# A GRU over 128 steps: the input products of the last four steps made plainly, with the input weights loaded a second time

## The chip, the cores and the metric

The kernel runs on one core of a Trainium2 chip. The core has TensorE (PE: matrix products, with PEld for loading the stationary operand), VectorE (DVE), ScalarE (ACT), GpSimd (POOL) and SyncE (SP, which here only issues DMAs). The metric is the device time of one execution in microseconds (us).

## The reference

`x` has 64 rows, 128 steps and 512 values; `h` starts as `cond_1024` (64 x 512). Everything is float32.

```python
def step(h, inp):
    x_t, prop = inp
    comb = jnp.concatenate([x_t, h], axis=-1)
    z = jax.nn.sigmoid(comb @ Wz + bz)
    r = jax.nn.sigmoid(comb @ Wr + br)
    comb2 = jnp.concatenate([x_t, r * h], axis=-1)
    h_cand = jnp.tanh(comb2 @ Wh + bh)
    h_new = (1.0 - z) * h + z * h_cand
    h_next = jnp.where(prop, jnp.tanh(h_new @ Wp + bp), h_new)
    return (h_next, h_new)
```

`prop` holds in every fourth step but the last one (steps 3, 7, ..., 123). The output is `x` plus the `h_new` of every step. Each of Wz, Wr, Wh has 1024 rows: the upper 512 multiply `x_t`, the lower 512 multiply `h` or `r * h`.

## The kernel before

**Layout.** The 64 rows and two halves of the 512 columns make 128 partitions: a state tile is 128 x 256. A product with a 512 x 512 weight is four k blocks of 128 (`K`), and each block is two matmuls, one for each half of the columns (`products`, L174, L177). I call one such pair of matmuls a unit. In the trace a float32 matmul leaves two records, so a unit leaves four. `ORDER` is 0, 2, 1, 3: the blocks of the first column half of the turned state come first.

**One step** (the loop at L557). The sums of R, Z and H live in PSUM slots, in two tiles: `rc` holds R and H, `zp` holds Z and the prop product. Each slot is seeded with the step's input part and bias by an ACT copy out of `G[t]` (`seed`, L382), and the h products add to it. The order on TensorE is: R (eight matmuls), Z (eight), the turns (transposes, L202, four records for each column half) of `rh`, x units from a queue (`fill`), H (eight, from `rhT`), x units, the turn of the new h's first half, x units, the second turn, x units. In a prop step the product with Wp, a second tanh and two more turns follow, again with x units between. Between these products stand: sigmoid on ACT (L598) and r*h on DVE (L599); the copies of turned tiles out of PSUM (L193); z, its complement and keep = (1-z)*h (L613 to L615); tanh on ACT (L637), times z (L638) and plus keep (L643) on DVE.

**The x part.** For steps 8 to 127 the products x @ W are made for eight steps at once (two groups of four steps) with two nested levels of a seven-product scheme for 2 x 2 blocks (Winograd's form of Strassen's). A group needs 49 products of 128 x 192 columns in place of 64. `batches` (L473) lists the 14 outer products of two groups and makes seven batches of two; a batch has 14 units. Their sums are read out of PSUM by ACT and DVE (`end_1`, `end_2`), and the outer sums that give `G[t]` are made on POOL (`outer_1` to `outer_c21`). The scheme's operands are sums: `sum_raw12` and its like make them from x on POOL, and those of the weights are made once, in steps 0 to 3, partly **in place** in `wx` (L304 to L314). After that `wx` no longer holds the input weights, except for its k block 3. Steps 1 to 7 use `plain` (L401): twelve units of 256 columns a step, read out by two DVE adds.

**What sets the order.** The program is written in the order in which each engine runs (`manual_schedule`). The number of x units at each place of a step is fixed by `PLACES`, with a period of eight steps: `fill(n)` takes n units from `queue`; a batch's read-out waits in `pending` until the next `read_out()`. The last call, `batches(30)` at step 114, covers groups 30 and 31 (steps 120 to 127); its 98 units are used up in step 122. Steps 123 to 127 have no x units. In step 127 half of Z is placed behind the turns of rh (L603 to L610).

**DMAs.** SP loads x group by group, turns it for TensorE by a DMA transpose (L253), and stores four steps of output at a time (L733).

Of the kernel before, what the change touches and what calls it, by code (L numbers as in the profile page):

```python
# [17 lines left out]
def kernel(  # L18
# [29 lines left out]
    nc = tc.nc  # L48
# [7 lines left out]
    Q4 = 4  # L56
    CHUNK = 4
    FIRST = 2
    R, Z, H_ = range(3)
    assert B * S == P and D == H and T % 8 == 0  # L60

# [93 lines left out]
    def cut(ps):  # L155
        return ps.rearrange("p (c n) -> p c n", c=C)
# [29 lines left out]
    def product(ps, lT, w, k, start=False):  # L186
        s0, c0 = divmod(k, C)
        products(ps, lT[:, c0, ts(s0, B)], lambda s: w[:, k, ts(s, N)], start)
# [37 lines left out]
    def turn_x(t, eng=nc.scalar):  # L226
        g, i = divmod(t, Q4)
        new_xT(g)
        src = xr[g] if g < 2 else early[g]
        for c in range(C):  # L230
            turn(src[:, i, :], xT[g][:, i], c, f"xT_{t}", eng)
# [96 lines left out]
    def sum_raw12(g):  # L328
        v = xT[g]
        sx[g, 12] = one.tile([P, 4, C, B], F32, tag="s12r", name=f"s12r_{g}")  # L330
        four([sx[g, 12][:, n] for n in range(4)], v[:, 0], v[:, 1])
# [6 lines left out]
    def sum_s12(g):  # L338
        v = xT[g]
        o = sx[g, "o12"] = one.tile([P, 2, 2, P], F32, tag="o12", name=f"o12_{g}")  # L340
        nc.gpsimd.tensor_add(o[:, 0], v[:, 2:4, 0, :], v[:, 2:4, 1, :])
        nc.gpsimd.tensor_sub(o[:, 1], o[:, 0], v[:, 0:2, 0, :])
        s = sx[g, 56] = one.tile([P, 4, 2, B], F32, tag="s56", name=f"s56_{g}")
        four([s[:, n] for n in range(4)], o[:, :, 0], o[:, :, 1])

    def sum_s34(g):
        v = xT[g]
        o = sx[g, "o34"] = one.tile([P, 2, 2, P], F32, tag="o34", name=f"o34_{g}")
        nc.gpsimd.tensor_sub(o[:, 0], v[:, 0:2, 0, :], v[:, 2:4, 0, :])
        nc.gpsimd.tensor_sub(o[:, 1], v[:, 0:2, 1, :], sx[g, "o12"][:, 1])  # L350
        s = sx[g, 73] = one.tile([P, 4, 2, B], F32, tag="s73", name=f"s73_{g}")
        four([s[:, n] for n in range(4)], o[:, :, 0], o[:, :, 1])
# [23 lines left out]
    def new_cp(q):  # L376
        if q not in cp:
            cp[q] = one.tile([P, C, 2, 3, P], F32, tag=f"cp{q % 2}", name=f"cp_{q}")
            for b in range(2):
                G[2 * q + b] = cp[q][:, :, b]  # L380

    def seed(i, t):  # L382
        if t < T:
            nc.scalar.copy(cut(slots[i]), G[t][:, :, i, :])  # L384
# [5 lines left out]
    def fill(n):  # L390
        for _ in range(min(n, len(queue))):
            unit, end = queue.pop(0)
            unit()
            if end is not None:
                pending.append(end)
# [5 lines left out]
    def plain(t):  # L401
# [20 lines left out]
        ]  # L422
        return [(u, None) for u in units[:-1]] + [(units[-1], end)]

    MB = {}

    def batch(n, ms):

        def region(ps, m):
            return ps[:, m].rearrange("p g u -> p (g u)")  # L430

        def unit(ps, m, j, start):
            g, i = ms[m]
            products(
                region(ps, m), lhs(g, i, j), lambda s: factor(i, j)[:, s], start and m == 0
            )

        def units(ps, j, start):
            return [lambda m=m: unit(ps, m, j, start) for m in range(2)]

        def blocks():
            return MB[n].rearrange("p m b g (a u) -> p m b a g u", a=2)

        def end_1():
            MB[n] = mbp.tile([P, 2, 2, 3, P], F32, tag="mb", name=f"mb_{ms[0][0]}_{ms[0][1]}")
            for m, (g, i) in enumerate(ms):
                M[g, i] = MB[n][:, m]
            T2[n] = one.tile([P, 2, 3, P // 2], F32, tag="cx", name=f"cx_{ms[0][0]}_{ms[0][1]}")
            q1 = one.tile([P, 2, 3, P // 2], F32, tag="cq", name=f"cq_{ms[0][0]}_{ms[0][1]}")
            nc.scalar.copy(T2[n], x_ps)  # L450
            nc.scalar.copy(q1, q_ps)
            nc.vector.tensor_add(T2[n], r_ps, T2[n])  # L452
            nc.vector.tensor_add(blocks()[:, :, 0, 0], a_ps, q1)

        def end_2():
            q2 = one.tile([P, 2, 3, P // 2], F32, tag="cq", name=f"cq2_{ms[0][0]}_{ms[0][1]}")
            nc.scalar.copy(q2, q_ps)  # L457
            nc.vector.tensor_add(blocks()[:, :, 0, 1], r_ps, q2)  # L458
            nc.vector.tensor_add(blocks()[:, :, 1, 0], x_ps, q2)
            nc.vector.tensor_add(blocks()[:, :, 1, 1], q_ps, T2[n])  # L460

        free = units(a_ps, 2, True)
        one_ = units(q_ps, 1, True) + units(r_ps, 5, True) + units(x_ps, 7, True)
        two_ = units(x_ps, 4, False) + units(q_ps, 6, False) + units(r_ps, 3, False)
        seq = [(u, None) for u in free + one_ + two_]
        seq[7] = (seq[7][0], end_1)
        seq[13] = (seq[13][0], end_2)
        return seq

    M = {}  # L470
# [2 lines left out]
    def batches(g):  # L473

        if g * Q4 >= T:
            return []
        ms = [(g, i) for i in (1, 2, 6, 5, 7, 3, 4)] + [(g + 1, i) for i in (1, 6, 2, 5, 3, 7, 4)]
        return sum((batch((g, n), ms[2 * n : 2 * n + 2]) for n in range(7)), [])


    def flat(v):
# [18 lines left out]
    def outer_1(g):  # L500
        with_bias(g, 1, bias0)
# [27 lines left out]
    )  # L529


    turn_x(0, nc.vector)
    turn_x(1, nc.vector)
    h = h_init
# [22 lines left out]
    for t in range(T):  # L557
# [7 lines left out]
        if t < 3:  # L565
            queue.extend(plain(2 * t + 2) + plain(2 * t + 3))
            places = (12, 12)
        elif t == 3:
            queue.extend(batches(FIRST))
            places = (8, 8, 6)  # L570
        elif u == 7:

            queue.extend(batches(even + 2))


        for k in ORDER:
# [11 lines left out]
            turn_x(2 * t + 6)  # L588
            turn_x(2 * t + 7)
        read_out()  # L590
        if u == 0 and pair >= 1:
            outer_u2(odd - 2)
        if t == 3:
            for i in (1, 2, 3):
# [5 lines left out]
        seed(R, t + 1)  # L600


        for k in ORDER[: 2 if last else K]:  # L603
            product(slots[Z], hT, wh[Z], k)
        rhT = new_T("rhT", f"rhT_{t}")
        for c in range(C):
            turn(rh, rhT, c, f"rhT_{t}", nc.vector)
        if last:
            for k in ORDER[2:]:
                product(slots[Z], hT, wh[Z], k)  # L610
        z = two.tile([P, N], F32, tag="z", name=f"z_{t}")
        keep = two.tile([P, N], F32, tag="keep", name=f"keep_{t}")
        nc.scalar.activation(z, slots[Z], AF.Sigmoid)  # L613
# [4 lines left out]
            nc.scalar.copy(cut(slot_p), bias[:, :, 3, :])  # L618
        if last:
            nc.gpsimd.tensor_add(xr[g][:, j, :], xr[g][:, j, :], keep)  # L620
        fill(places[0])


        for k in ORDER:
# [10 lines left out]
        for c in range(C):  # L635
# [5 lines left out]
                nc.vector.tensor_add(o, pc, o)  # L641
                continue
            nc.vector.tensor_add(h_new[:, ts(c, P)], pc, keep[:, ts(c, P)])  # L643
        seed(H_, t + 1)
        read_out()
        fill(places[1] - 3 if places[1] > 6 else 4)
        h = h_new
        if not last:
            hT = new_T("hT", f"hT_{t}")
            turn(h, hT, 0, f"hT_{t}", nc.vector)  # L650
            fill(1)
            turn(h, hT, 1, f"hT_{t}", nc.scalar)
        fill(2 if places[1] > 6 else 1)
        if t == 2:
            sum_outer_1()
        if t == 3:
# [2 lines left out]
        if prop:  # L659
            for k in ORDER:  # L660
                product(slot_p, hT, wp, k)
            read_out()
            h = two.tile([P, N], F32, tag="hprop", name=f"hprop_{t}")
            for c in range(C):
                nc.scalar.activation(h[:, ts(c, P)], slot_p[:, ts(c, P)], AF.Tanh)
            fill(places[2] - 2)
            hT = new_T("hT", f"hpT_{t}")
            for c in range(C):
                turn(h, hT, c, f"hpT_{t}", (nc.vector, nc.scalar)[c])
            fill(2)  # L670
        if t == 0:
            turn_x(4)
            turn_x(5)
# [3 lines left out]


        if pair >= 0:
            if u == 0 and pair >= 1:  # L680
                outer_c22(odd - 2)
                outer_c21(odd - 2)
            if here:
                if u == 0:
                    sum_s34(even)
                    outer_1(even)
                elif u == 1:
                    outer_c11(even)
                    sum_raw12(odd)
                elif u == 2:  # L690
                    outer_u1(even)
                    outer_5(even)
                    sum_raw4(even)
                elif u == 3:
                    outer_c12(even)
                    outer_u2(even)
                    outer_c22(even)
                    sum_s12(odd)
                elif u == 4:
                    outer_c21(even)  # L700
                    outer_1(odd)
                    sum_s34(odd)
                elif u == 5:
                    outer_u1(odd)
                    outer_c11(odd)
                    sum_raw4(odd)
                elif u == 7:
                    outer_5(odd)
                    outer_c12(odd)
        if u == 7 and pair >= -1 and (even + 2) * Q4 < T:  # L710
# [11 lines left out]
            nc.gpsimd.tensor_add(xr[g][:, j, :], xr[g][:, j, :], h_new)  # L722


        n = 0
        if t >= T - CHUNK:
            n = {T - 2: 3, T - 1: 1}.get(t, 0)
# [60 lines left out]
```

## Time and profile before

| | us |
|---|---|
| median of 3 runs (lowest to highest) | 1371.43 (1371.06 to 1373.5) |
| profiled execution, device time | 1370.75 |
| its span, first to last instruction | 1368.9 |
| TensorE busy | 1342.6 |
| GpSimd busy | 938.7 |

The last steps, each counted from its first R product to the next step's (the last one to the end of the span), with the x units placed in it:

| step | start | length | x units |
|---|---|---|---|
| 117 | 1262.27 | 9.67 | 12 |
| 118 | 1271.94 | 8.56 | 8 |
| 119 (prop) | 1280.50 | 14.09 | 20 |
| 120 | 1294.59 | 8.44 | 8 |
| 121 | 1303.03 | 8.44 | 8 |
| 122 | 1311.47 | 9.88 | 12 |
| 123 (prop) | 1321.35 | 11.53 | 0 |
| 124 | 1332.88 | 8.44 | 0 |
| 125 | 1341.32 | 8.44 | 0 |
| 126 | 1349.76 | 8.44 | 0 |
| 127 | 1358.20 | 10.70 | 0 |

A timeline line reads: start, duration of the merged group, engine, line and operation, output<-input, shape, how many records; in brackets, how long the engine sat idle before it and what released it. The ends of matmuls are modelled, so lengths on TensorE are best read from start to start. In the slices, a digit is the busy share of one fortieth of the span in tenths.

### The profile page before, as it was taken

How to read it: one execution, taken by the hardware profiler on the slowest of the kernel's cores; microseconds unless marked ns; L12 is line 12 of the kernel's file. 1: busy time of each engine (PE TensorE's matmuls, PEld its weight loads, DVE VectorE, ACT ScalarE, POOL GpSimd, SP SyncE). 2: the span in 40 equal slices, each digit the busy share in tenths (PEclk: the TensorE clock that was granted, in tenths of full speed). 3: DMA queues.
4: the chain of work that ended last, by engine and by line, in shares of the span. 5: the costliest groups of instructions: out<-in, count | busy, mean ns of one | idle time of the engine just before them, and what ended most of it. 6: DMA issues, size and time to landing. Idle time of an engine off the chain costs nothing.

```text
span 1368.9 us, 37448 instructions
## 1 busy us (share of the span) xinstructions
PE 1342.6 (98%) x15336; PEld 1028.9 (75%) x15336; DVE 689.2 (50%) x1875; ACT 631.2 (46%) x1857; POOL 938.7 (69%) x1139
## 2 busy tenths in 40 slices
PE   7999999999999999999999999999999999999996
PEld 4777777777777777777777777777777777777764
DVE  4245554555555555554555555555555555555543
ACT  1234445445444445445445444445445445454443
POOL 4327676787767786677686767786677686767740
PEclk9999999999999999999999999999999999999999
DMA  9002212212231222212222131222212222131010
GB/s 286 11 17 48 63 32 63 63 33 63 49 77 32 60 36 63 63 32 63 52 43 63 43 83 34 49 46 63 63 32 63 48 48 63 35 76 33 17 33 16
DMA packets 113572, 73.86 MB, mean 54 GB/s; under 512 B 61556, under 2 KB 109812, under 8 KB 113400
## 3 DMA queue, kind: packets, MB, share of 16 engines
q1 hardware_dynamic: 112336, 69.68, 22.5%
q8 instruction: 121, 1.98, 0.6%
q10 hardware_dynamic: 1064, 1.78, 0.4%
q14 instruction: 51, 0.42, 0.1%
HBM read 39.99 MB, written 16.78 MB: 41 GB/s over the span
## 4 chain that ended last, share of the span: by engine, by line
PE 96%; DMA 2%; DVE 1%; ACT 0%; issue 0%; SPq 0%; DVEq 0%; ACTq 0%
PE rc L177 33%; PE zp L177 20%; PE scratch_q L177 11%; PE scratch_x L177 10%; PE scratch_r L177 10%; PE turn L202 6%; PE scratch_a L177 6%; DMA early<-in_x_dram 1%; DMA wx<-in_L_cond_Wz_dram 1%; DMA wh<-in_L_cond_Wr_dram 1%; DVE h L643 0%; DVE turn L638 0%; ACT xT L193 0%; SPq L93 0%; DVE tw L300 0%
## 5 line engine op out<-in xcount | busy, mean ns | idle before, releaser
L177 PE MATMUL rc<-wh,rhT 128*64 128x256 f32 x2048 | 246.6, 381 | 2.0 <-ACT zp L614 2.0
L485 POOL TENSOR_TENSOR cp<-mb,mb 128x768 f32<-128x768 f32 x75 | 136.6, 1821 | 112.1 <-ACT rc L384 67.1
L177 PEld LDWEIGHTS rc<-wh,rhT 128*64 128x64 f32 x2048 | 158.9, 137 | 55.0 <-ACT zp L614 12.4
L177 PE MATMUL rc<-wh,hT 128*64 128x256 f32 x1536 | 183.1, 380 | 0.5 <-DVE hT L193 0.2
L177 PE MATMUL zp<-wh,hT 128*64 128x256 f32 x1536 | 183.2, 379 | 0.0
L722 POOL TENSOR_TENSOR xr<-xr,h 128x256 f32<-128x256 f32 x127 | 92.5, 729 | 102.1 <-DVE h L643 95.5
L193 DVE COPY rhT<-turn 128x256 uint16<-128x256 uint16 x256 | 96.8, 420 | 127.1 <-PE turn L202 127.1
L638 DVE TENSOR_TENSOR turn<-turn,z 128x128 f32<-128x128 f32 x256 | 75.5, 295 | 161.0 <-ACT turn L637 161.0
L485 POOL TENSOR_TENSOR cp<-mb 128x768 f32<-128x768 f32 x45 | 81.9, 1820 | 108.4 <-ACT rc L384 107.2
L177 PEld LDWEIGHTS zp<-wh,hT 128*64 128x64 f32 x1536 | 117.5, 137 | 47.4
L177 PEld LDWEIGHTS rc<-wh,hT 128*64 128x64 f32 x1536 | 111.6, 137 | 45.2 <-issue 1.0
L598 ACT ACTIVATE turn<-rc 128x128 f32<-128x128 f32 x256 | 55.4, 260 | 156.6 <-issue 85.6
L452 DVE TENSOR_TENSOR cx<-scratch_r,cx 128x384 f32<-128x384 f32 x105 | 58.6, 558 | 128.7 <-ACT cx L450 128.7
L193 ACT COPY hT<-turn 128x256 uint16<-128x256 uint16 x127 | 47.3, 373 | 155.8 <-PE turn L202 96.6
L485 POOL TENSOR_TENSOR mb<-mb,mb 128x768 f32<-128x768 f32 x60 | 109.2, 1820 | 13.4 <-DVE mb L460 13.4
L458 DVE TENSOR_TENSOR mb<-scratch_r,cq 128x384 f32<-128x384 f32 x105 | 58.6, 558 | 88.1 <-ACT cq L457 88.1
L384 ACT COPY rc<-cp 128x256 f32<-128x256 f32 x254 | 95.8, 377 | 11.6 <-POOL s L325 0.4
L637 ACT ACTIVATE turn<-rc 128x128 f32<-128x128 f32 x256 | 57.0, 262 | 90.3 <-PE rc L177 90.3
L613 ACT ACTIVATE z<-zp 128x256 f32<-128x256 f32 x128 | 49.2, 384 | 104.0 <-PE zp L177 104.0
L202 PEld LDWEIGHTS <-h 128*64 128x64 bf16 x1016 | 47.4, 109 | 51.0 <-DVE h L643 46.0
L384 ACT COPY zp<-cp 128x256 f32<-128x256 f32 x127 | 47.9, 377 | 78.1 <-DVE keep L615 78.1
L202 PE MATMUL turn<-ident,h 128*64 128x128 bf16 x1016 | 76.6, 227 | 5.4 <-DVE h L643 5.4
(149 smaller groups left out, 2954.6 us busy)
## 6 DMA issues: line engine op xcount, KB each, us to landing
xr<-in_x_dram SPq DMA_DIRECT2D x62, 256.0 KB, 4.2
out_dram<-xr SPq DMA_DIRECT2D x62, 256.0 KB, 3.3
xs<-in_x_dram SPq DMA_DIRECT2D x56, 256.0 KB, 4.3
wh<-in_L_cond_Wr_dram SPq DMA_DIRECT2D x2, 512.0 KB, 7.6
wh<-in_L_cond_Wz_dram SPq DMA_DIRECT2D x2, 512.0 KB, 8.3
wh<-in_L_cond_Wh_dram SPq DMA_DIRECT2D x2, 512.0 KB, 10.4
early<-in_x_dram SPq DMA_DIRECT2D x4, 256.0 KB, 13.1
wp<-in_L_cond_Wp_dram SPq DMA_DIRECT2D x1, 1024.0 KB
```

Of the source, the lines that this page charges most:

```text
L177: nc.tensor.matmul(ps[s * B : (s + 1) * B], lhsT=lhs, rhs=rhs(s), start=start, stop=True, skip_group_check=True,)
L193: (eng.copy if eng is nc.scalar else eng.tensor_copy)(dst, src)
L202: nc.tensor.transpose(pt[s * B : (s + 1) * B, w, :], words.rearrange("p (n w) -> p w n", w=2)[:, w, :], ident16,)
L384: nc.scalar.copy(cut(slots[i]), G[t][:, :, i, :])
L452: nc.vector.tensor_add(T2[n], r_ps, T2[n])
L458: nc.vector.tensor_add(blocks()[:, :, 0, 1], r_ps, q2)
L485: nc.gpsimd.tensor_add(dst, a, b)
L598: nc.scalar.activation(act_ps[c], slots[R][:, ts(c, P)], AF.Sigmoid)
L613: nc.scalar.activation(z, slots[Z], AF.Sigmoid)
L637: nc.scalar.activation(pc, slots[H_][:, ts(c, P)], AF.Tanh)
L638: nc.vector.tensor_mul(pc, pc, z[:, ts(c, P)])
L722: nc.gpsimd.tensor_add(xr[g][:, j, :], xr[g][:, j, :], h_new)
```

## The change

`batches(30)` now covers group 30 alone: seven outer products in four batches, the last of one product. Group 31 (steps 124 to 127) gets no scheme. Its sums on POOL, its operand sums and its read-outs are gone. In step 118 SP loads the three changed k blocks of `wx` again from memory (nine DMAs). `plain_last` queues 48 plain units in step 119, those of the untouched k block 3 first, then k blocks 1, 0, 2; each step's sums are read out by two DVE adds. In steps 119 to 127 (`thin`) the number of units at each place is set by `TAIL`; none stand between the turns of rh and H any more, and Z's last two units stand one behind each turn of rh. The H seed of step 127 moves from step 126 into step 127.

```diff
+    LAST = T // Q4 - 1
...
+    def plain_last():
+        def units(t, gates, first_k):
+            first, second = scratch[:2] if t % 2 == 0 else scratch[2:]
+            regions = (first[:, :N], first[:, N:], second[:, :N])
+            return [
+                lambda e=e, k=k: product(
+                    regions[e], xT[LAST][:, t % Q4], wx[:, :, e, :], k, k == 3 and e != Z
+                )
+                for k in first_k
+                for e in gates
+            ]
+
+        def end(t, gates):
+            first, second = scratch[:2] if t % 2 == 0 else scratch[2:]
+            new_cp(t // 2)
+            if R in gates:
+                nc.vector.tensor_add(
+                    G[t][:, :, 0:2, :],
+                    first.rearrange("p (g c n) -> p c g n", g=2, c=C),
+                    bias[:, :, 0:2, :],
+                )
+            if H_ in gates:
+                nc.vector.tensor_add(
+                    G[t][:, :, 2, :], cut(second[:, :N]), bias[:, :, 2, :]
+                )
+
+        t0 = LAST * Q4
+        seq = [(u, None) for t in (t0, t0 + 1) for u in units(t, (R, Z, H_), (3,))]
+        for t in (t0, t0 + 1):
+            us = units(t, (R, Z, H_), (1, 0, 2))
+            seq += [(u, None) for u in us[:-1]] + [(us[-1], lambda t=t: end(t, (R, Z, H_)))]
+        for t, gates in ((t0 + 2, (R, Z, H_)), (t0 + 3, (R, Z)), (t0 + 3, (H_,))):
+            us = units(t, gates, (3, 1, 0, 2))
+            seq += [(u, None) for u in us[:-1]] + [(us[-1], lambda t=t, g=gates: end(t, g))]
+        return seq
+
+    def reload():
+        for k in (1, 0, 2):
+            for i in range(3):
+                load_w(wx[:, :, i, :], gates_in[i], k, k + 1, nc.sync)
...
-        ms = [(g, i) for i in (1, 2, 6, 5, 7, 3, 4)] + [(g + 1, i) for i in (1, 6, 2, 5, 3, 7, 4)]
-        return sum((batch((g, n), ms[2 * n : 2 * n + 2]) for n in range(7)), [])
+        ms = [(g, i) for i in (1, 2, 6, 5, 7, 3, 4)]
+        if g + 1 < LAST:
+            ms += [(g + 1, i) for i in (1, 6, 2, 5, 3, 7, 4)]
+        return sum((batch((g, n), ms[2 * n : 2 * n + 2]) for n in range(7) if 2 * n < len(ms)), [])
...
+    TAIL = (
+        ((4, 1, 0), (2, 1)), ((4, 1, 0), ()), ((4, 1, 0), ()), ((4, 1, 0), ()),
+        ((4, 1, 0), (2, 1)), ((4, 1, 0), ()), ((5, 1, 2), ()), ((3, 1, 0), ()), ((0, 0, 0), ()),
+    )
...
+        thin = t >= T - 9
+        if thin:
+            places, behind = TAIL[t - (T - 9)]
+            if t == T - 9:
+                assert not queue
+                queue.extend(plain_last())
+        if t == T - 10:
+            places = (4, 6)
+            assert len(queue) == 7
...
+        if t == T - 1:
+            seed(H_, t)
...
-        for k in ORDER[: 2 if last else K]:
+        for k in ORDER[: 2 if thin else K]:
             product(slots[Z], hT, wh[Z], k)
         rhT = new_T("rhT", f"rhT_{t}")
         for c in range(C):
             turn(rh, rhT, c, f"rhT_{t}", nc.vector)
-        if last:
-            for k in ORDER[2:]:
-                product(slots[Z], hT, wh[Z], k)
+            if thin:
+                product(slots[Z], hT, wh[Z], ORDER[2 + c])
...
-        fill(places[0])
+        if not thin:
+            fill(places[0])
...
-        seed(H_, t + 1)
+        if t < T - 2:
+            seed(H_, t + 1)
         read_out()
-        fill(places[1] - 3 if places[1] > 6 else 4)
+        fill(places[0] if thin else places[1] - 3 if places[1] > 6 else 4)
...
-            fill(1)
+            fill(places[1] if thin else 1)
             turn(h, hT, 1, f"hT_{t}", nc.scalar)
-        fill(2 if places[1] > 6 else 1)
+        fill(places[2] if thin else 2 if places[1] > 6 else 1)
...
-            fill(places[2] - 2)
+            fill(behind[0] if thin else places[2] - 2)
...
-            fill(2)
+            fill(behind[1] if thin else 2)
...
+        if t == T - 10:
+            reload()
```

The parts left out make the read-outs of a batch work for one product (`[:, :nm]`) and skip the sums of group 31.

More of the change, by code (lines that the diff above doesn't have):

```diff
@@ L438, in units @@
         def units(ps, j, start):
-            return [lambda m=m: unit(ps, m, j, start) for m in range(2)]
+            return [lambda m=m: unit(ps, m, j, start) for m in range(len(ms))]
         def blocks():
@@ L447, in end_1 @@
                 M[g, i] = MB[n][:, m]
+            nm = len(ms)
             T2[n] = one.tile([P, 2, 3, P // 2], F32, tag="cx", name=f"cx_{ms[0][0]}_{ms[0][1]}")
             q1 = one.tile([P, 2, 3, P // 2], F32, tag="cq", name=f"cq_{ms[0][0]}_{ms[0][1]}")
[L450 to L453, printed above, removed]
+            nc.scalar.copy(T2[n][:, :nm], x_ps[:, :nm])
+            nc.scalar.copy(q1[:, :nm], q_ps[:, :nm])
+            nc.vector.tensor_add(T2[n][:, :nm], r_ps[:, :nm], T2[n][:, :nm])
+            nc.vector.tensor_add(blocks()[:, :nm, 0, 0], a_ps[:, :nm], q1[:, :nm])
         def end_2():
             q2 = one.tile([P, 2, 3, P // 2], F32, tag="cq", name=f"cq2_{ms[0][0]}_{ms[0][1]}")
[L457 to L460, printed above, removed]
+            nm = len(ms)
+            nc.scalar.copy(q2[:, :nm], q_ps[:, :nm])
+            nc.vector.tensor_add(blocks()[:, :nm, 0, 1], r_ps[:, :nm], q2[:, :nm])
+            nc.vector.tensor_add(blocks()[:, :nm, 1, 0], x_ps[:, :nm], q2[:, :nm])
+            nc.vector.tensor_add(blocks()[:, :nm, 1, 1], q_ps[:, :nm], T2[n][:, :nm])
         free = units(a_ps, 2, True)
@@ L465, in batch @@
         seq = [(u, None) for u in free + one_ + two_]
-        seq[7] = (seq[7][0], end_1)
-        seq[13] = (seq[13][0], end_2)
+        for n_units, end in ((4 * len(ms), end_1), (7 * len(ms), end_2)):
+            seq[n_units - 1] = (seq[n_units - 1][0], end)
         return seq
@@ L590 @@
         read_out()
-        if u == 0 and pair >= 1:
+        if t == T - 1:
+            seed(H_, t)
+        if u == 0 and pair >= 1 and odd - 2 < LAST:
             outer_u2(odd - 2)
@@ L679 @@
         if pair >= 0:
-            if u == 0 and pair >= 1:
+            if u == 0 and pair >= 1 and odd - 2 < LAST:
                 outer_c22(odd - 2)
@@ L688 @@
                     outer_c11(even)
-                    sum_raw12(odd)
+                    if odd < LAST:
+                        sum_raw12(odd)
                 elif u == 2:
@@ L697 @@
                     outer_c22(even)
-                    sum_s12(odd)
+                    if odd < LAST:
+                        sum_s12(odd)
                 elif u == 4:
                     outer_c21(even)
-                    outer_1(odd)
-                    sum_s34(odd)
-                elif u == 5:
+                    if odd < LAST:
+                        outer_1(odd)
+                        sum_s34(odd)
+                elif u == 5 and odd < LAST:
                     outer_u1(odd)
@@ L706 @@
                     sum_raw4(odd)
-                elif u == 7:
+                elif u == 7 and odd < LAST:
                     outer_5(odd)
```

## The prediction

> **What bounds the kernel now.** I read the page's head first, then the engine rows and the slices, then TensorE's timeline over the last steps, then the same stretches cut step by step.
>
> ```profile
> span 1368.9 us, 37448 instructions
> PE 1342.6 (98%) x15336; PEld 1028.9 (75%) x15336; DVE 689.2 (50%) x1875; ACT 631.2 (46%) x1857; POOL 938.7 (69%) x1139
> PE   7999999999999999999999999999999999999996
> ```
>
> TensorE is full in every slice but the first and the last. Only a stretch where it is not full can give time without less work, and that is the last slice. Busy time and clock in the stretches of steps 120, 121, 124 and 125 (columns: length, then busy us and instruction count of PE, PEld, DVE, ACT, POOL, granted clock, DMA share, GB/s):
>
> ```profile
> 1294.59:1303.03 8.44, 8.44 (x99) 6.35 (x98) 4.49 (x13) 3.08 (x11) 4.11 (x5) 1.00 0.43 108
> 1303.03:1311.47 8.44, 8.44 (x100) 6.25 (x98) 4.02 (x12) 3.84 (x13) 2.98 (x7) 1.00 0.09 19
> 1332.88:1341.32 8.44, 6.46 (x64) 4.14 (x65) 3.00 (x10) 2.77 (x11) 0.40 (x1) 1.00 0.14 30
> 1341.32:1349.76 8.44, 6.46 (x65) 4.61 (x65) 3.00 (x10) 3.03 (x11) 0.73 (x2) 1.00 0.01 2
> ```
>
> A step with eight x units and a step with none take the same 8.44 us. So a plain step is bound by its chain (R, sigmoid, r*h, turn, H, tanh, new h, turn), and eight units fit into the chain's holes. TensorE in step 125 and then in step 127:
>
> ```profile
> 1341.32 1.95 PE L177 MATMUL rc<-wh,hT 128*64 128x256 f32 x16
> 1343.07 1.93 PE L177 MATMUL zp<-wh,hT 128*64 128x256 f32 x16
> 1344.80 0.42 PE L202 MATMUL turn<-ident,rh 128*64 128x128 bf16 x8
> 1345.72 1.95 PE L177 MATMUL rc<-wh,rhT 128*64 128x256 f32 x16 [0.50 <-ACT zp L614]
> 1348.81 0.31 PE L202 MATMUL turn<-ident,h 128*64 128x128 bf16 x4 [1.14 <-DVE h L643]
> 1349.34 0.31 PE L202 MATMUL turn<-ident,h 128*64 128x128 bf16 x4 [0.22 <-DVE h L643]
> 1349.76 1.95 PE L177 MATMUL rc<-wh,hT 128*64 128x256 f32 x16
> ...
> 1358.20 1.95 PE L177 MATMUL rc<-wh,hT 128*64 128x256 f32 x16
> 1359.94 1.06 PE L177 MATMUL zp<-wh,hT 128*64 128x256 f32 x8
> 1360.87 0.50 PE L202 MATMUL turn<-ident,rh 128*64 128x128 bf16 x8
> 1361.20 1.03 PE L177 MATMUL zp<-wh,hT 128*64 128x256 f32 x8
> 1362.07 1.90 PE L177 MATMUL rc<-wh,rhT 128*64 128x256 f32 x16
> ```
>
> Prices from start to start: sixteen records of 256 columns take 1.725 us (0.108 each), so a plain unit (two products, four records) costs 0.431. A batch unit (four records of 192 columns) takes 0.325: in step 121, 1309.13 to 1309.78 is two of them. A turn of four records is 0.11. A step's own work is 3 x 1.725 + 0.45 = 5.63 us; a step with the prop product has 1.95 more.
>
> The chain in two halves: **R to H** is 1345.72 - 1341.32 = 4.40, and **end of H to the next R** is 1349.76 - 1347.45 = 2.31 (1.36 until h is there for its first turn, then 0.95 of turn, DVE copy of hT and hand-over). In step 127 R to H is only 3.87, because half of Z lies behind the turns and covers the copy of rhT. H there starts at 1362.07 although L614 runs only at 1362.57, so the "ACT zp L614" named in step 125 is not what H waits for; the rhT copy that starts at 1345.14 and lasts 0.42 is.
>
> **The change part by part.**
>
> *TensorE's work.* Up to step 117 nothing on TensorE differs: batches 0 to 2 of the last call hold the same products, and 7 units are left at step 118 instead of 56. The 56 cost 56 x 0.325 = 18.2 us; now 7 x 0.325 + 48 x 0.431 = 23.0. So **4.8 us more work**, which has to fit into holes.
>
> How big are the holes? The busy row says 8.44 - 6.46 = 1.98 us in step 125. The Trainium skill, Perfetto Trace Analysis, section Identifying the Most-Contended Engine, says that matmul busy time is no good measure, because the instructions are pipelined. The start-to-start count agrees with it: 8.44 - 5.63 = 2.81. By the busy row five units (2.16) would not fit, a step would be 6.46 + 2.16 = 8.62, and steps 119 to 126 together would be some 4.5 us longer than in the sum below (0.48 in each of four plain steps, 0.73 in two prop steps, 1.2 in steps 125 and 126), no gain left. By the count they fit. I take the count.
>
> *Z parted by the turns, steps 119 to 127.* R 1.74, two Z units 0.86; the first turn then waits for r*h, which in step 127 lets it start 2.67 after R; turn 0.11, Z 0.43, turn 0.11, Z 0.43: H could start at 3.75. The rhT copy for the first half starts 0.35 after its turn and takes 0.42, ready at 3.5, so hidden. The second half's turn is at 3.2, its copy is ready at some 4.1, and H needs it two units (0.86) after 3.75. Bounds: 3.63 (pure work) to 4.40 (as now); I take **3.75**, next to the row 3.87. z, keep and the z seed come 0.27 us later than in step 125; they were there 2 us before L643 needs them.
>
> *The fill after H, (4,1,0).* Four plain units take 1.725, longer than the 1.36 that h needs, so the first turn slips to 1.725 and its copy with it: next R at 1.725 + 0.94 = **2.665**. The fifth unit (0.43) is hidden in those 0.94. Pure work would be 2.38; with nothing overlapped it would be 2.31 + 2.16 = 4.47. The step's DVE and ACT queues hold no more than now, so I stay at 2.665.
>
> A thin step is then 3.75 + 1.725 + 2.665 = 8.14. In the prop steps 119 and 123 the prop product adds 1.73, and its fill (2,1) gives 0.86 + 0.88 = 1.74 to the next R (0.88 is turn to R in step 119 now): 11.61. Step 125 with (5,1,2): after H 2.155 + 0.11 + 0.43 + 0.11 + 0.86 = 3.67, so 9.15. Step 126 with (3,1,0): 1.36 + 0.95, so 7.78.
>
> *Step 118, (4,6).* Four units instead of two ahead of H: 1.73 + 1.73 + 0.23 + 1.30 = 4.99; then only three units left, 1.36 + 0.95 = 2.31 behind H: 9.02 against 8.56. The single batch's first read-out is moved ahead of tanh on ACT: two copies of half width, some 0.45 us, in front of the two xT joins (1.40); tanh would be free at 1278.9, and H ends at 1278.65 + 0.31. Nothing, or 0.1.
>
> *The reads of the plain sums.* Two DVE adds a step, 0.68 and 0.42 by the rows of steps 2 to 7 (L409, L414), queued ahead of r*h. Their units are done before or during R, which gives 2.3 us of cover; without it each would delay r*h by up to 1.1. The four step parts together take 4.4 us on DVE where seven eighths of four batch read-outs (20 adds of 0.56) go away. On ACT the H seed of step 127 goes behind step 127's R, with 1.7 us before the sigmoid. POOL loses nine adds of 1.82 and the group's sums, 26 us in all; TensorE waits for none of them in this stretch, so nothing.
>
> *The reload.* Nine loads of 256 KB, 2.36 MB, on SP's queue in step 118, ahead of the store of step 119. wx is last read at the end of step 117 (1271.9; the one batch of step 118 reads tw and tt only). SP is idle then.
>
> ```profile
> xr<-in_x_dram SPq DMA_DIRECT2D x62, 256.0 KB, 4.2
> GB/s 286 11 17 48 63 32 63 63 33 63 49 77 32 60 36 63 63 32 63 52 43 63 43 83 34 49 46 63 63 32 63 48 48 63 35 76 33 17 33 16
> ```
>
> SP's timeline has two such loads issued in 1.30 us, so nine in 5.9; at the first slice's 286 GB/s the data take 8.3, so all are there by about 1284. The skill (DMA: Bandwidth & Descriptors, section Bandwidth) speaks against pieces this small: it wants 1 MiB and gives 138 GB/s at 64 KB and 341 at 1 MB. At 138 the estimate is 17 us, 1289. The first product of a reloaded plane is unit 7, in step 119 behind prop, at about 1291; plane 2 is first used at 1300. Hidden either way.
>
> **The sum.** 9.02 + 2 x 11.61 + 4 x 8.14 + 9.15 + 7.78 = 81.7 us for steps 118 to 126, against 1358.20 - 1271.94 = 86.26: -4.5. Step 127 gains 3.87 - 3.75 = 0.1. Together **-4.7 us**: span 1364.2, profiled execution 1370.75 to 1366.1. The median of the runs is 0.7 above the profiled one, so **1366.7**, 0.34% faster.
>
> **The rivals.**
>
> *The parted Z saves nothing.* If r*h's turns in the middle of Z held TensorE so that H came at 4.40 as now, eight steps would be 0.65 longer: 1366.7 + 5.2 = 1371.9, no change. Against it stands step 127, where the same products in nearly this order gave 3.87.
>
> *The units after H cost more than the gap.* If h or hT is late behind them by 0.3 us in each of eight steps (DVE or ACT out of turn), 2.4 of the gain is lost: 1369.1. Against it: the filled step 120 has turn to R at 1.00, the empty one 0.95.
>
> *The reload is late, and the kernel slower.* If the first plain product (step 119 behind H, 1286.4) waits for the whole reload, not its own plane, lateness goes straight onto the path. At 108 GB/s, the rate of the busiest tail stretch above, the data take 22 us and land at 1294 to 1296: a stall of about 9, giving 1376. Nine in a row at 4.2 us each would be 1309.7 and 1390. It decides from about 1294 on (7.4 late: the gain plus 0.2%). Against it: the loads are issued 0.65 apart and overlap at the start of the kernel.
>
> **How the numbers follow.** Main case 0.78, the first rival 0.08, the second 0.07, the late reload 0.07. A measurement can tell about 0.2% (2.7 us) from no change. The main case's own range is 1364.6 to 1369: down by half of the 4.1 us of holes still left in the sum (81.7 less 54.6 + 23.0 of work), up by a late copy here and there. With the second rival in, and the spread of the runs (0.4 below the median, more above), it is 1364.2 to 1369.9. Faster 0.80, within 0.2% 0.13, slower 0.07.
>
> **What would show it.** R to H at 3.7 to 3.8 in steps 119 to 127; R to R 8.1 in steps 120 to 122 and 124; about 9.0 in step 118; the wait ahead of R named as the DVE hT copy, some 0.3; no wait of TensorE for wx. Wrong if H still comes at 4.4, if the first turn after H comes later than 1.75 behind it, or if a product of scratch waits for a DMA.

## The result and the profile after

The changed kernel takes **1367.42 us** (median of 7 runs, 1366.69 to 1368.81) against 1371.43 for the kernel before (1370.83 to 1373.5): a ratio of **0.9969, 95% interval 0.9957 to 0.9981**. The medians differ by 4.0 us, about 0.3%; 1366.7 was forecast.

The head of the page of the changed kernel, its engine row and its slices for TensorE:

```profile
span 1365.7 us, 37407 instructions
PE 1346.4 (99%) x15332; PEld 1025.1 (75%) x15332; DVE 686.6 (50%) x1868; ACT 626.2 (46%) x1848; POOL 912.2 (67%) x1110
PE   7999999999999999999999999999999999999998
```

TensorE is busy 3.8 us longer in a span that is 3.2 us shorter, and the last slice rose from 6 to 8. Work was added and a shorter time came out, which can only be had from time in which TensorE had stood idle. The stretches of steps 120, 121, 124 and 125 (length, then busy us and count of PE, PEld, DVE, ACT, POOL, granted clock, DMA share, GB/s):

```profile
1293.34:1301.50 8.16, 8.09 (x85) 5.25 (x85) 3.28 (x10) 2.68 (x11) 0.73 (x1) 1.00 0.28 75
1301.50:1309.65 8.15, 8.08 (x85) 5.54 (x85) 3.42 (x11) 3.03 (x11) 0.73 (x1) 1.00 0.01 2
1329.38:1337.81 8.43, 8.21 (x85) 5.24 (x85) 3.42 (x11) 2.68 (x11) 0.69 (x1) 1.00 0.04 10
1337.81:1347.02 9.21, 9.21 (x97) 6.38 (x99) 4.07 (x12) 3.37 (x11) 0.77 (x2) 1.00 0.01 2
```

Steps 119 to 126 all carry x units now, and all of them but step 124 come within 0.1 us of the length that was worked out. TensorE in step 121 and in step 127:

```profile
1301.50 1.95 PE L178 MATMUL rc<-wh,hT 128*64 128x256 f32 x16
1303.25 1.06 PE L178 MATMUL zp<-wh,hT 128*64 128x256 f32 x8
1304.18 0.31 PE L203 MATMUL turn<-ident,rh 128*64 128x128 bf16 x4
1304.32 0.60 PE L178 MATMUL zp<-wh,hT 128*64 128x256 f32 x4
1304.75 0.28 PE L203 MATMUL turn<-ident,rh 128*64 128x128 bf16 x4
1304.86 0.60 PE L178 MATMUL zp<-wh,hT 128*64 128x256 f32 x4
1305.30 1.90 PE L178 MATMUL rc<-wh,rhT 128*64 128x256 f32 x16
...
1308.75 0.28 PE L203 MATMUL turn<-ident,h 128*64 128x128 bf16 x4
1308.86 0.60 PE L178 MATMUL scratch_x<-wx,xT 128*64 128x256 f32 x4
1309.29 0.28 PE L203 MATMUL turn<-ident,h 128*64 128x128 bf16 x4
1309.65 1.95 PE L178 MATMUL rc<-wh,hT 128*64 128x256 f32 x16
...
1354.77 1.95 PE L178 MATMUL rc<-wh,hT 128*64 128x256 f32 x16
1356.52 1.06 PE L178 MATMUL zp<-wh,hT 128*64 128x256 f32 x8
1357.84 0.31 PE L203 MATMUL turn<-ident,rh 128*64 128x128 bf16 x4 [0.27 <-DVE rh L667]
```

In step 121, R to H is 1305.30 - 1301.50 = 3.80, where it was 4.40 in the steps without units, and the turns of h are followed by R at 1309.65, 2.62 behind the end of H. In step 127 the first turn of rh has to wait for r*h, which it did not in step 121. I come back to that line.

Step by step, in us:

| | forecast | changed kernel | kernel before |
|---|---|---|---|
| step 118 | 9.02 | 8.92 | 8.56 |
| step 119 (prop) | 11.61 | 11.58 | 14.09 |
| steps 120, 121, 122 | 8.14 each | 8.16, 8.15, 8.14 | 8.44, 8.44, 9.88 |
| step 123 (prop) | 11.61 | 11.59 | 11.53 |
| step 124 | 8.14 | 8.43 | 8.44 |
| step 125 | 9.15 | 9.21 | 8.44 |
| step 126 | 7.78 | 7.75 | 8.44 |
| sum of 118 to 126 | 81.7 | 81.93 | 86.26 |
| step 127, R to H | 3.75 | 4.19 | 3.87 |

The two spans differ by only 3.2 us because step 118 begins 0.9 later in the profiled execution of the changed kernel (1272.84 against 1271.94), although TensorE's work up to there is the same. Over all ten profiles of this study that start lies between 1271.75 and 1273.13. So for the experiments I use, beside the run times, one length that leaves it out: the **tail**, from the first R product of step 118 to the first H product of step 127. It is 90.13 before and 86.12 after, a difference of 4.01.

### The profile page after: what moved, and what is told of

Read it like the earlier page. It is cut to its first block, busy times and chain, and to the rows that moved or that the text cites. A ratio compares the mean times of both kernels' runs of the same rounds, so it can differ in the third digit from the quotient of the medians.

```text
span 1365.7 us, 37407 instructions
## 1 busy us (share of the span) xinstructions
PE 1346.4 (99%) x15332; PEld 1025.1 (75%) x15332; DVE 686.6 (50%) x1868; ACT 626.2 (46%) x1848; POOL 912.2 (67%) x1110
## 3 DMA queue, kind: packets, MB, share of 16 engines
q8 instruction: 121, 1.98, 0.6%
## 4 chain that ended last, share of the span: by engine, by line
PE 98%; DVE 1%; ACT 0%; issue 0%; DMA 0%; ACTq 0%; DVEq 0%
PE rc L178 33%; PE zp L178 20%; PE scratch_q L178 11%; PE scratch_x L178 10%; PE scratch_r L178 10%; PE scratch_a L178 6%; PE turn L203 6%; DVE tw L302 0%; DVE tw L301 0%; DMA tt<-in_L_cond_bh_dram 0%; ACT xT L194 0%; PE rc L161 0%; PE zp L161 0%; ACT xT L264 0%; DVE rh L667 0%
## 5 line engine op out<-in xcount | busy, mean ns | idle before, releaser
L534 POOL TENSOR_TENSOR cp<-mb,mb 128x768 f32<-128x768 f32 x72 | 130.8, 1817 | 106.5 <-ACT rc L385 64.3
L706 DVE TENSOR_TENSOR turn<-turn,z 128x128 f32<-128x128 f32 x256 | 75.4, 295 | 156.3 <-ACT turn L705 156.2
L534 POOL TENSOR_TENSOR mb<-mb,mb 128x768 f32<-128x768 f32 x58 | 105.4, 1817 | 11.5 <-DVE mb L507 11.5
L385 ACT COPY rc<-cp 128x256 f32<-128x256 f32 x254 | 95.6, 376 | 13.3 <-PE rc L178 1.7
L385 ACT COPY zp<-cp 128x256 f32<-128x256 f32 x127 | 47.8, 377 | 77.5 <-DVE keep L682 77.5
L711 DVE TENSOR_TENSOR h<-turn,keep 128x128 f32<-128x128 f32 x254 | 74.1, 292 | 15.4
```

The source lines that it names most:

```text
L534: nc.gpsimd.tensor_add(dst, a, b)
L706: nc.vector.tensor_mul(pc, pc, z[:, ts(c, P)])
```

## The experiments

The theory was that the gain is made of two things, the parted Z (0.65 us of R to H) and the x units laid into the holes, less 4.8 us of added work. The main rivals were that one of the two does it alone, and that the reload costs something.

Each ratio is to runs of the kernel before on the same chip.

| run | tail | median | ratio to before (95%) |
|---|---|---|---|
| before | 90.13 | | |
| changed kernel | 86.12 | 1367.42 | 0.9969 (0.9957 to 0.9981) |
| Z whole | 90.97 | 1372.27 | 1.0001 (0.9992 to 1.001) |
| kernel before with Z parted | 87.57 | 1368.41 | 0.9976 (0.9966 to 0.9986) |
| no reload | 86.12 | 1367.49 | 0.9965 (0.9952 to 0.9977) |
| H seed behind the sigmoids | 85.64 | 1367.78 | 0.9965 (0.9952 to 0.9978) |
| places (3, 1, 1) | 85.03 | 1366.78 | 0.9965 (0.9952 to 0.9977) |
| both of these | 84.62 | 1367.21 | 0.9968 (0.9955 to 0.998) |
| changed kernel again | 86.10 | 1367.58 | 0.9969 (0.9956 to 0.9981) |

**Z whole, all else as changed.**

```diff
-        for k in ORDER[: 2 if thin else K]:
+        for k in ORDER[: 2 if last else K]:
...
-            if thin:
+            if last:
                 product(slots[Z], hT, wh[Z], ORDER[2 + c])
```

> The changed kernel, but Z stands whole ahead of the turns of rh in steps 119 to 126 (step 127 keeps its parted Z). My theory: the parted Z is worth 4.40 - 3.75 = 0.65 us in each of eight steps, so R to H goes back to 4.4, a thin step to 8.8, and the whole to about 1367.4 + 5.2 = 1372.6, all of the gain gone. Rival (the gain comes from spreading the x units over the holes, and the parting adds little): R to H rises by less than 0.2 and the time stays within 1.5 us of 1367.4.

Measured: 1372.27, no different from the kernel before. TensorE in step 121 of this kernel:

```profile
1301.68 1.95 PE L178 MATMUL rc<-wh,hT 128*64 128x256 f32 x16
1303.43 1.93 PE L178 MATMUL zp<-wh,hT 128*64 128x256 f32 x16
1305.16 0.42 PE L203 MATMUL turn<-ident,rh 128*64 128x128 bf16 x8
1306.08 1.95 PE L178 MATMUL rc<-wh,rhT 128*64 128x256 f32 x16 [0.50 <-ACT zp L681]
```

R to H is 4.40 again, with the 0.50 of idle time ahead of H, and steps 120 to 122 and 124 take 8.79 each. Without the parted Z, then, moving the units to the holes and making them plainly gives nothing: the tail is 0.84 longer than before. The rival that spreading does it alone has fallen. The work that the change takes off POOL, DVE and ACT is gone in this run too, so it does not give the gain by itself either.

**Only the parted Z, in the kernel before.**

```diff
-        for k in ORDER[: 2 if last else K]:
+        parted = t >= T - 5
+        for k in ORDER[: 2 if parted else K]:
             product(slots[Z], hT, wh[Z], k)
...
             turn(rh, rhT, c, f"rhT_{t}", nc.vector)
-        if last:
-            for k in ORDER[2:]:
-                product(slots[Z], hT, wh[Z], k)
+            if parted:
+                product(slots[Z], hT, wh[Z], ORDER[2 + c])
```

> The kernel before, with one edit: Z's last two units stand one behind each turn of rh in steps 123 to 127. No x unit is moved, nothing is loaded again. My theory: R to H falls from 4.40 to 3.75 in steps 123 to 126 and from 3.87 to 3.75 in step 127, the next R follows H by 2.31 as before, a step takes 7.8: 1371.4 - 2.7 = 1368.7, more than half of the change's gain without its added work. Rival (the holes must be filled with x units for a gain): no difference beyond 0.5 us.

Measured: 1368.41, tail 2.56 shorter than before. R to H is 3.79 or 3.80 in steps 123 to 127, and the waits for h stay as they were. TensorE in step 125 of this kernel, with its H and the turns of h behind it:

```profile
1340.14 1.95 PE L177 MATMUL rc<-wh,hT 128*64 128x256 f32 x16
...
1343.93 1.90 PE L177 MATMUL rc<-wh,rhT 128*64 128x256 f32 x16
1346.98 0.31 PE L202 MATMUL turn<-ident,h 128*64 128x128 bf16 x4 [1.15 <-DVE h L643]
1347.51 0.31 PE L202 MATMUL turn<-ident,h 128*64 128x128 bf16 x4 [0.22 <-DVE h L643]
```

A move of two units in five steps, with no reload and no added work, is worth 2.6 of the 4.0 us. The rest, 1.45 us, is read from the tails; the intervals of the two ratios overlap, so the run times do not tell this simpler kernel from the changed one.

The two runs do not add up: units and places alone cost 0.84, the parting alone gives 2.56, both together give 4.01. The difference is 2.3 us. Set beside the kernel with Z whole, the changed kernel saves 2.57 us in steps 119 to 122, which the second run did not touch, and 2.29 in steps 123 to 127, where the second run saved 2.55. In the kernel before, x units stand between the turns and H in steps 119 to 122 and cover the copy of rhT. TensorE there in step 121, with no idle time ahead of H:

```profile
1306.48 0.40 PE L202 MATMUL turn<-ident,rh 128*64 128x128 bf16 x8
1306.71 0.83 PE L177 MATMUL scratch_x<-tt,o 128*64 128x192 f32 x8
1307.38 1.95 PE L177 MATMUL rc<-wh,rhT 128*64 128x256 f32 x16
```

So the parting should have nothing to shorten there until the units are moved away; that it gives nothing with the units in place was not run.

**No reload.**

```diff
-        if t == T - 10:
-            reload()
```

> The changed kernel without the second load of the input weights; the plain products of the last four steps then use weights that were changed in place, so the x part of those steps is left out of what the kernel gets right. My theory: the nine loads are there 10 us before the first plain product and hide, so the tail's steps keep their lengths within 0.05 us and the time stays at 1367.4 within the spread of the start (0.9). Rival (the transfers disturb other engines or hold the first plain product): a shorter step 118 or 119, 0.5 us or more.

Measured: every step from 118 to 126 within 0.01 of the changed kernel's, tail 86.12 in both. The reload costs nothing. In the changed kernel the issues on SP's queue read (the first and the last of nine), and on TensorE the first plain product and the first one of a reloaded block:

```profile
1268.36 0.37 SPq L99 DMA_DIRECT2D wx<-in_L_cond_Wr_dram  x1
...
1272.09 0.43 SPq L99 DMA_DIRECT2D wx<-in_L_cond_Wh_dram  x1
```

```profile
1287.27 1.03 PE L178 MATMUL scratch_q<-wx,xT 128*64 128x256 f32 x8
...
1292.08 0.63 PE L178 MATMUL scratch_q<-wx,xT 128*64 128x256 f32 x4
```

The last issue is at 1272.09 and the longest of the nine takes 6.1 us to land, so all is there by 1278.2: 9 us ahead of the first plain product (1287.27, of the untouched block), 14 ahead of the first product of a reloaded one (1292.08).

**The H seed of step 127 behind the sigmoids.**

```diff
-        if t == T - 1:
-            seed(H_, t)
...
         seed(R, t + 1)
+        if t == T - 1:
+            seed(H_, t)
```

> The changed kernel, with the ACT copy that seeds H in step 127 placed behind the two sigmoids of r instead of ahead of them. My theory: that copy waits for the end of R and delays the sigmoid by 0.4; behind the sigmoids it is hidden, R to H in step 127 falls from 4.19 to 3.75 and the stretch from step 127's first R to the end of the span from 10.93 to about 10.5. Rival (the sigmoid is late for another reason, as it was by 0.25 in step 124, where no seed stands ahead of it): R to H stays above 4.0.

ACT in step 127, first in the changed kernel, then in this one:

```profile
1354.71 0.37 ACT L194 COPY hT<-turn 128x256 uint16<-128x256 uint16 x1 [1.51 <-PE turn L203]
1356.80 0.38 ACT L385 COPY rc<-cp 128x256 f32<-128x256 f32 x1 [1.71 <-PE rc L178]
1357.20 0.43 ACT L666 ACTIVATE turn<-rc 128x128 f32<-128x128 f32 x2
```

```profile
1356.12 0.43 ACT L664 ACTIVATE turn<-rc 128x128 f32<-128x128 f32 x2 [1.66 <-PE rc L178]
1356.59 0.38 ACT L385 COPY rc<-cp 128x256 f32<-128x256 f32 x1
```

In the changed kernel ACT stands idle for 1.71 us ahead of the seed (L385): the seed waits for the end of R, and the sigmoid that R releases at the same moment stands behind it. Counted from R, the sigmoid comes at 1357.20 - 1354.77 = 2.43 there and at 1356.12 - 1354.14 = 1.98 here. R to H falls from 4.19 to 3.74 as expected, and R to the end of the span from 10.93 to 1364.7 - 1354.14 = 10.56. The median, 1367.78, can't show 0.4 us.

**The same seed ahead of R**, with the read-out that feeds it, to see why it waits for R.

```diff
+        if t == T - 1:
+            read_out()
+            seed(H_, t)
         for k in ORDER:
             product(slots[R], hT, wh[R], k)
...
         read_out()
-        if t == T - 1:
-            seed(H_, t)
```

> The changed kernel with the read-out of the last plain unit and the H seed of step 127 ahead of step 127's R products. Two explanations of why the seed waited for R: (a) the order of the program alone, since R and H lie in one PSUM tile and whichever is written second waits for the first: then R now waits for the seed and begins some 0.5 to 0.7 later behind H than the 2.27 of now, with R to H at 3.75; (b) the read-out is late: then the seed is still late and R to H stays at 4.2.

TensorE of this kernel:

```profile
1354.37 0.28 PE L203 MATMUL turn<-ident,h 128*64 128x128 bf16 x4
1355.53 1.95 PE L178 MATMUL rc<-wh,hT 128*64 128x256 f32 x16 [0.88 <-ACT rc L385]
```

Explanation (a) holds: now R waits for the seed, begins 3.04 behind H in place of 2.27, and R to H is 3.82. The seed and R lie in one PSUM tile, `rc`, in different halves, and still the later one in the program waits for the earlier one. A single run took 1368.34, and its tail is 86.51, 0.4 longer than the changed kernel's.

**Three units behind H in place of four.**

```diff
-        ((4, 1, 0), (2, 1)), ((4, 1, 0), ()), ((4, 1, 0), ()), ((4, 1, 0), ()),
-        ((4, 1, 0), (2, 1)), ((4, 1, 0), ()), ((5, 1, 2), ()), ((3, 1, 0), ()), ((0, 0, 0), ()),
+        ((3, 1, 1), (2, 1)), ((3, 1, 1), ()), ((3, 1, 1), ()), ((3, 1, 1), ()),
+        ((3, 1, 1), (2, 1)), ((3, 1, 1), ()), ((5, 1, 2), ()), ((3, 1, 0), ()), ((0, 0, 0), ()),
```

> The changed kernel with (3, 1, 1) in place of (4, 1, 0) in steps 119 to 124: three x units behind H, one between the turns of h, one behind them; nothing else moves. My theory: the fourth unit behind H makes the first turn 0.37 late and the copy of hT with it; with three the turn comes at 1.36, the two other units lie in the copy's time, and the end of H to the next R falls from 2.62 to about 2.4. Six steps by 0.2: about 1.3 us, 1366.1. Rival (R waits for the copy either way, since it is the copy that ends last): 2.6 stays, no difference.

TensorE in step 121 of this kernel, from H to the next R:

```profile
1304.04 1.90 PE L178 MATMUL rc<-wh,rhT 128*64 128x256 f32 x16
...
1307.09 0.31 PE L203 MATMUL turn<-ident,h 128*64 128x128 bf16 x4
1307.22 0.60 PE L178 MATMUL scratch_a<-wx,xT 128*64 128x256 f32 x4
1307.66 0.28 PE L203 MATMUL turn<-ident,h 128*64 128x128 bf16 x4
1307.77 0.60 PE L178 MATMUL scratch_x<-wx,xT 128*64 128x256 f32 x4
1308.20 1.90 PE L178 MATMUL rc<-wh,hT 128*64 128x256 f32 x16
```

The first turn is 1.32 behind H (it was 1.73) and R follows at 2.44, with TensorE full in between. The same in steps 119, 120, 123 and 124; in step 122 it stayed at 2.61, because there one DVE multiply (L706) starts 0.2 later than in the other steps. It does so in the changed kernel too, where the fourth unit hides it; I have no cause for it. The tail is 1.09 shorter where 1.3 was expected: 0.9 of it lies between H and R, and 0.2 in R to H, which fell from 3.80 to 3.75 in steps 121, 122, 123 and 125. The ratio of the runs, 0.9965, can't be told from the 0.9969 of the changed kernel on the same chip.

**Both edits together**: the H seed behind the sigmoids and (3, 1, 1).

> The changed kernel with both: (3, 1, 1) in steps 119 to 124, and the H seed of step 127 behind the sigmoids. My theory: 1.3 + 0.4 = 1.7 us less, 1365.7, a ratio to the kernel before of about 0.9957. Rival: as for the edit of the places alone, 0.4 us only.

The tail is the shortest of all, 84.62, so 1.5 below the changed kernel's and 5.5 below the kernel before. The median is 1367.21, between those of the two edits alone, where 1365.7 was expected: a gain of 1.5 is in the profile, but the runs (interval 0.9955 to 0.998) don't show that this version beats the changed kernel.

**The changed kernel again**, as the base of these.

> The changed kernel once more, unaltered, beside the two others on the same chip, as their base: 1367.4, ratio 0.997.

It came out at 1367.58, with the same step lengths to 0.02 us, the late ones in steps 124 and 127 among them.

## Why the prediction was right

- **What bounds the tail.** A chain with holes, not TensorE's work. Right: with 3.8 us more busy time the kernel is 4.0 us faster. The count from start to start was the one to go by: a step with five units takes 8.15, where the busy row would have made it 8.62. The busy row read too much (6.46 us for 5.63 of work in the empty step), because the records of neighbouring groups overlap: a row of 1.95 us is followed by the next one after 1.75.
- **Z parted, R to H at 3.75.** 3.79 to 3.81 in most steps. The two runs that add or take away this part alone move R to H by 0.6 in most steps, where the prediction had 0.65. The first rival (no gain from it) has fallen.
- **The fill (4,1,0), end of H to R at 2.665.** 2.62, held by the copy of hT behind a late first turn, as worked out; putting one unit elsewhere took 0.2 off. The prediction wanted to see a wait of 0.3 named for that copy; none of TensorE's rows here names one, since the modelled end of the last turn leaves 0.08 us. The copy itself shows it: in step 121 it ends at 1309.50 and R follows 0.15 later, and in step 125 of the kernel before it ends at 1349.61, again 0.15 ahead of R. DVE's copies, first in the changed kernel, then before:

```profile
1309.08 0.42 DVE L194 COPY hT<-turn 128x256 uint16<-128x256 uint16 x1 [0.26 <-PE turn L203]
```

```profile
1349.20 0.41 DVE L193 COPY hT<-turn 128x256 uint16<-128x256 uint16 x1
```

  The second rival (units cost more than the gap) did not come about.
- **Step 118, the prop steps, 125, 126.** Within 0.1 each.
- **The reload.** Hidden, and by more than I had. I took its issue to wait for the end of step 117 because a product there still reads wx (scratch_r<-wx,s, 1272.5). That product reads k block 3, which is not loaded again, so the loads began at 1268.36, 4.5 us ahead of that step's end. SP issued nine in 4.2 us (5.9 were reckoned), and the data were there within 10 us of the first issue. The prediction's slower estimate was 17 us, from the 138 GB/s that the Trainium skill (DMA: Bandwidth & Descriptors, section Bandwidth) gives for a transfer of 64 KB issued from GpSimd. These were nine loads of 256 KB from SP, in flight together, so the estimate does not hold for them, and the page's row was not tested. The late-reload rival has fallen too.
- **Step 127: wrong in sign.** "On ACT the H seed of step 127 goes behind step 127's R, with 1.7 us before the sigmoid" failed. The seed waits for R, through the shared PSUM tile, and holds the sigmoid. R to H was 4.19 instead of 3.75. I had named what was queued behind the seed but not asked what the seed itself would wait for.
- **Step 124: 0.3 too long.** R to H was 4.08. The sigmoid comes 2.32 behind R instead of 2.04, so r*h is late for the first turn. The wait on ACT's queue ahead of it is as long as in the kernel before, 2.02 us from R's start. ACT's waits ahead of the sigmoid in step 124 of the changed kernel, then of the kernel before:

```profile
L666 ACTq EVENT_SEMAPHORE  x1: 2022/2022/2022, 1329.4 to 1329.4; - x1
```

```profile
L598 ACTq EVENT_SEMAPHORE  x1: 2021/2021/2021, 1332.9 to 1332.9; - x1
```

  And the sigmoids behind these waits:

```profile
1331.70 0.43 ACT L666 ACTIVATE turn<-rc 128x128 f32<-128x128 f32 x2 [2.32 <-PE rc L178]
```

```profile
1334.92 0.43 ACT L598 ACTIVATE turn<-rc 128x128 f32<-128x128 f32 x2 [1.98 <-PE rc L177]
```

  The wait ends at about 1331.4, the sigmoid starts at 1331.70; before, it started at 1334.92, less than 0.1 behind the wait. So ACT loses some 0.3 between the end of the wait and the instruction. It does so at this place in every kernel of this study that has the plain sums, in the one with Z whole as well, where the last of Z hides it. The traces have one lead: in each of these eight kernels a load of instructions (8 KB, DMA queue 14) begins 0.63 to 0.66 us behind the start of this sigmoid, at 1332.35 in the changed kernel, and such a load follows the late L706 of step 122 as well (1315.74, 0.69 behind it, with places (3, 1, 1)). But in the kernel before one follows the sigmoid of step 121 at the same distance (1305.67), and that sigmoid is not late (1.99 behind R). So the cause stays open.

The two misses, +0.3 and +0.4, make up the 0.7 us by which the tail missed its forecast (86.12 against 81.7 + 3.75). That the median missed by the same 0.7 is partly luck, since the start of step 118 alone moves by 1.4 us between profiles.

## What to carry to other kernels

Where a chain of waits bounds a stretch, look first for independent work on the same engine that can be placed inside a wait, in the order in which it helps the next hand-over: here two units of Z behind the turns gave 2.6 us in five steps, and moving the x units gave nothing without them. In this kernel filling the holes paid only with the chain itself made shorter, and a unit ahead of a hand-over beyond what the wait covered made the hand-over late. For an instruction that is moved, ask what it will wait for in its new place, down to the tile that it shares with others, before asking who waits behind it.

## What was not expected of the hardware

- The seed's and R's instructions work on different halves of one PSUM tile and still wait for each other in program order (ACT idle for 1.71 us in one order, TensorE for 0.88 in the other). Whether the memory needs that order, or only the program asks for it, was not tried.
- The same work on TensorE reaches step 118 at times from 1271.75 to 1273.13. This spread, 1.4 us, is larger than what the late seed (0.5) or the places (1.1) gain alone and about as large as both together (1.5), so a single profile's span can't show them.
- Nine 256 KB loads, 2.36 MB, landed within 10 us of the first issue and changed no step by more than 0.01 us, with TensorE busy all the time from 1268 to 1280.
